# One h2T copy moved from ScalarE to VectorE, and one block of gate weights turned behind the messages of graph 1, in a two-layer graph network

## The chip, the cores and the metric

The kernel runs on one core of one Trainium2 chip. The metric is the device time of one execution in microseconds (us). In the three timed runs of the kernel before it was 2075.66, 2078.24 and 2078.29 us, median 2078.24 us. The engines are called PE (TensorE), ACT (ScalarE), DVE (VectorE), POOL (GpSimd) and SP (SyncE, which here only issues transfers); PEld is TensorE's weight load.

## The reference, cut to what matters

There are 64 graphs of 256 nodes with 256 features, all float32. `x` is (64, 256, 256), `adj` is (64, 256, 256).

```python
# layer 0
h = relu(layernorm(x))
x = x + relu(norm(adj + I) @ h @ W.T + b)
# layer 1, with h2 = relu(layernorm(x))
x_conv = relu(bn2(conv2_17_taps(relu(bn1(conv1(h2))))) + h2)
A      = exp(-dist(h2 @ w_se.T + b_se)) * adj
x_nmp  = A @ relu(h2 @ w_msg.T + b_msg)
gi     = concat(x_conv, x_nmp) @ w_ih.T + b_ih
gh     = h2 @ w_hh.T + b_hh
x = x + GRU_gates(gi, gh, h2)
```

[...] 

## The kernel before, in words

The kernel has three stages. In the first, all graphs pass through layer 0 and the first products of layer 1: `turn_adj`, `aggregate`, `project`, `turn_h`, `messages`, `conv1`, then for pairs of graphs `turn_cols`, `distance` and `pass_messages`. Beside that the weights are made ready. Then come the products of the 17-tap convolution in a transformed domain, and the gates.

Graphs 0 to 3 go through the first stage in a list written out by hand, `begin()` (lines 1165 to 1242); from graph 4 on a loop does it (line 1285). All engines keep the order of the program. Each engine's order is set by when the Python code makes its instruction: PE's instructions are made on the spot; what follows a product on another engine is put off by `after(beats, go)` (line 247) and made when `beat()` (line 559) has been called so many times more. A `beat()` also feeds the work that is paced, of which there is none this early.

These are the functions around the change:

- `turn_h(g, at, by)` (line 993): four 128x128 turns of `h2` on PE into a bank `ht`; `at` beats later `keep` copies the bank to `h2T`, and SP issues a store of it (`hTd`). `keep` uses ACT if `by` is given or paced work is waiting, else DVE.
- `messages(g)` (line 1041): eight 128x259 products `ms` from `h2T` into a bank of its own that ACT has filled with the bias first (`own_bank`, line 1014); after that DVE copies three columns (`cols`) and ACT makes `mso`. ACT fills the bank for the next graph two beats later.
- `conv1(g)` (line 1030): eight products `c` from `h2T` into another such bank, then ACT's `c1o` and a store `h1d`.
- `gate_load` and `load_part` (lines 752 and 599), called `L(w, o0)`: SP loads 256 rows of a gate matrix to a tile `nat`. `gate_turn` and `turn_away` (lines 755 and 626), called `T(w, o0)`: PE turns them, four 128x128 turns a bank, `evict` copies each bank to `w_wi` or `w_wh` (in `begin()` always on ACT), and SP stores it. `turn_away` calls `beat(0.4)` once a bank: twice for `w_ih`, once for `w_hh`. `WI` is `w_ih`, `WH` is `w_hh`.
- `later` (line 770): a list of lists of such jobs; `begin()` takes the first list between graphs 1 and 2. It is `TL(0)`, which is `taps_load` (line 645), and `L(WH, 2)`. `TL(0)` and `TL(1)` are the two loads of the raw convolution weights `w2n`, 2176 KB each, and the only loads that POOL issues. The second list gives `TL(1)`.
- `project(g)` (line 934): after its products, DVE's `pre` and `x` rows, a store `x2d`, the moments on DVE, `rs` and `nmr` on POOL, and the rows of `h2` on ACT (`norm`), two halves one beat apart.
- `load(g)` (line 819): loads of `x` and `adj` for a pair of graphs, 512 KB each.

SP issues every other load and store, one after the other in the order of the program. The program gives these transfers eight semaphores in turn, so each waits until the eighth transfer before it has landed. The tiles `nat` of 256 columns have two buffers.

The turn of the first 256 rows of `w_hh`, tile `t_wh`, stands on PE between `c` of graph 2 and `ht` of graph 3, both before and after the change.

Of the kernel before, what the change touches and what calls it, by code (L numbers as in the profile page):

```python
# [185 lines left out]
def gnn_kernel(  # L186
# [24 lines left out]
    def scratch(name, shape):  # L211
# [29 lines left out]
    pe, act, vec, pool, sp = (  # L241
        Pinned(tc, e) for e in (nc.tensor, nc.scalar, nc.vector, nc.gpsimd, nc.sync)
    )
# [3 lines left out]
    def after(beats, go):  # L247
        due.append([beats, go])

    def come_due():  # L250
        now = []
        for d in list(due):
            d[0] -= 1
            if d[0] < 0:
                now.append(d[1])
                due.remove(d)
        for go in now:
            go()
# [288 lines left out]
    with ExitStack() as one:  # L547
# [11 lines left out]
        def beat(us):  # L559
            come_due()  # L560
            paced.issue(*(k * us for k in share))

        def bank(name):
            return ps.tile([P, 512], FP, tag="ps", name=name)
# [41 lines left out]
        def turn_part(dst, nat, o0, i, tag, scale=None):  # L606

            if scale is not None:
                for k in range(2):
                    act.mul(nat[:, k, :], nat[:, k, :], scale[:, o0 + k : o0 + k + 1])  # L610
            for i0 in range(0, i // P, 2):
                t = bank(f"t_{tag}_{i0}_{o0}")
                for q in range(2):
                    for k in range(2):
                        pe.transpose(
                            t[:, (q * 2 + k) * P : (q * 2 + k + 1) * P],
                            nat[:, k, (i0 + q) * P : (i0 + q + 1) * P],
                            ident,
                        )
                after(0, lambda t=t, i0=i0: evict(  # L620
                    dst[:, i0 : i0 + 2, o0 * P : (o0 + 2) * P],
                    t.rearrange("p (q m) -> p q m", q=2),
                ))
                beat(0.4)
# [127 lines left out]
        def gate_load(tag, src, o0, i):  # L752
            nat[tag, o0] = load_part(src, o0, i, tag)

        def gate_turn(tag, dst, o0, i):
            turn_away(dst, nat.pop((tag, o0)), o0, i, tag)

        WI = ("wi", w_ih, 2 * D)
        WH = ("wh", w_hh, D)
        L = lambda w, o0: (lambda: gate_load(w[0], w[1], o0, w[2]))  # L760
        T = lambda w, o0: (lambda: gate_turn(w[0], wi_d if w is WI else wh_d, o0, w[2]))
# [75 lines left out]
        def row_moments(g, rows):  # L837
            xt, _ = st[g]["both"]
            if "mv" not in st[g]:
                st[g]["mv"] = small.tile([P, NR, 2], FP, tag="mv0", name=f"mv0_{g}", bufs=1)  # L840
            for r in rows:
                s6 = small.tile([P, 6], FP, tag="st", name=f"st0_{g}_{r}")
                vec.bn_stats(s6, xt[:, r, :])
                vec.bn_aggr(st[g]["mv"][:, r, :], s6)
# [53 lines left out]
        def turn_adj(g, at=(1, 2), by=pool):  # L898
            s = st[g]
            t = bank(f"at_{g}").rearrange("p (c i) -> p c i", c=NB)  # L900
            for jc in range(NB):
                for ic in range(NB):
                    pe.transpose(
                        t[:, jc, ic * P : (ic + 1) * P], s["at"][:, ic, jc * P : (jc + 1) * P], ident
                    )

            def keep():
                s["adjT"] = work.tile([P, NB, N], FP, tag="adjT", name=f"adjT_{g}", bufs=6)
                act.copy(s["adjT"], t)

            def hat():
                s["adjH"] = work.tile([P, NB, N], FP, tag="adjH", name=f"adjH_{g}")
                by.tensor_tensor(s["adjH"], s["adjT"], eye, ALU.add)
            after(at[0], keep)
            if at[1] is None:
                return hat
            after(at[1], hat)

        def aggregate(g):
            s = st[g]  # L920
            t = bank(f"ag_{g}").rearrange("p (c i) -> p c i", c=DC)
            for fc in range(DC):
                for jc in range(NB):
                    pe.matmul(
                        t[:, fc, :], s["hs"][:, jc, fc * P : (fc + 1) * P], s["adjH"][:, jc, :],
                        start=(jc == 0), stop=(jc == NB - 1),
                    )

            def keep():
                s["aggT"] = work.tile([P, DC, N], FP, tag="aggT", name=f"aggT_{g}")  # L930
                act.copy(s["aggT"], t)
            after(1, keep)
# [60 lines left out]
        def turn_h(g, at=1, by=None):  # L993
            s = st[g]
            t = bank(f"ht_{g}").rearrange("p (c i) -> p c i", c=DC)
            for dc in range(DC):
                for nb in range(NB):
                    pe.transpose(
                        t[:, dc, nb * P : (nb + 1) * P],
                        s["h2"][:, nb, dc * P : (dc + 1) * P],  # L1000
                        ident,
                    )

            def keep():
                s["hT"] = work.tile([P, DC, N], FP, tag="h2T", name=f"h2T_{g}")

                (act.copy if by or any(paced.lines) else vec.tensor_copy)(s["hT"], t)
                nc.sync.dma_start(hT_d[g].rearrange("p (c n) -> p c n", c=DC), s["hT"])
            after(at, keep)
# [144 lines left out]
        def stats(b):  # L1154

            g, rows = b // G * G, range(b % G * NB, (b % G + 1) * NB)
            degrees(g, rows, lambda: row_moments(g, rows))

        def scale_rows(b):
            factors(b // G * G, range(b % G * NB, (b % G + 1) * NB))  # L1160

        def rows_in(b):
            layer0_in(b // G * G, range(b % G * NB, (b % G + 1) * NB))

        def begin():

            weights_by[:] = [act.copy]
            stats(0)
            turn_adj(0, (0, 0))
            beat(0.4)  # L1170
            scale_rows(0)
            turn_part(w0T, nat_w0, 0, D, "w0")
            hat = turn_adj(1, (0, None), vec)
            beat(0.4)
            stats(1)
            hat()
            scale_rows(1)
            rows_in(0)
            turn_adj(2, (0, 0))
            beat(0.4)  # L1180
            stats(2)
            rows_in(1)
            aggregate(0)
            beat(1.7)
            turn_adj(3, (0, 1))
            scale_rows(2)
            beat(0.4)
            stats(3)
            rows_in(2)
            turn_part(wmT, nat_wm, 0, D, "wm")  # L1190
            aggregate(1)
            scale_rows(3)
            row_moments(2 * G, range(NR))
            degrees(2 * G)
            beat(1.7)
            project(0)
            beat(1.7)
            rows_in(3)
            T(WI, 0)()
            L(WI, 4)()  # L1200
            factors(2 * G)
            aggregate(2)
            beat(1.7)
            project(1)
            beat(1.7)
            small_turns()
            beat(0.1)
            aggregate(3)
            beat(1.7)
            turn_adj(4)  # L1210
            own_bank("ms", 0, bmB)
            beat(0.4)
            project(2)
            beat(1.7)
            turn_h(0, 0, act)
            small_shift()
            beat(0.4)
            turn_part(w1T, nat_w1, 0, D, "w1", scale=sc[:, 0:DC])
            own_bank("c1", 0, b1B)
            load(3 * G)  # L1220
            project(3)
            beat(1.7)
            messages(0)
            beat(1.7)
            layer0_in(2 * G, range(2))
            conv1(0)
            beat(1.7)
            T(WI, 2)()
            L(WH, 0)()
            turn_h(1, 0, act)  # L1230
            beat(0.4)
            for go in later.pop(0):
                go()
            layer0_in(2 * G, range(2, NR))
            beat(0.4)
            messages(1)
            beat(1.7)
            later.pop(0)[1]()
            later[2].insert(0, T(WI, 4))
            conv1(1)  # L1240
            beat(1.7)
            weights_by[:] = []
# [39 lines left out]
        FILTER, SPECTRA, PRODUCTS = 2, 7, 4  # L1282
        filtering = []
        begin()
        for n in range(4, B + 5):
            even, odd = n % G == 0, n % G == 1
# [391 lines left out]
```

## Time and profile before

| what | value |
|---|---|
| median of three timed runs | 2078.24 us |
| the profiled execution's own time | 2076.19 us |
| its span, first to last instruction | 2074.4 us |
| PE busy | 2029.9 us, 98% of the span |
| DVE, ACT, POOL busy | 68%, 48%, 53% |
| mean granted clock of TensorE | 0.997 |
| idle time of PE in the hundred us from 0 to 100 | 10.9 us |
| time of the change | 37 to 48 us after the span's start |

The profile is of one execution. A timeline row gives an instruction's start, its length, its engine, the line, the operation, and out<-in; rows of the same kind are merged with their number, and behind them stands how long the engine had been idle and what ended that. Nearly all instructions carry line 102, since a helper makes them, so they are told apart by the names of their tiles. The view by windows gives, for each stretch, the busy time of each engine, the granted clock of TensorE (1.00 is full) and the share of the time that the 16 DMA engines were busy.

### The profile page before, as it was taken

Reading aid. Unit: us, or ns where it says so; the run is one execution under the profiler, and the core shown is the slowest. Engines: PE = TensorE matmul, PEld = TensorE weight load, DVE = VectorE, ACT = ScalarE, POOL = GpSimd, SP = SyncE. Lnnn points to the kernel's source line nnn. Section 1 sums busy time; section 2 is a strip of 40 time slices with the busy share of each in tenths; the row PEclk is TensorE's granted clock in tenths of the full one; section 3 lists DMA queues with packets and bytes.
Section 4 is the critical chain, followed back from the end, with each engine's and each line's share of the span. In section 5 each row is a group of like instructions: output and inputs, shape, how many; then the busy total and the mean of one; then the engine's idle time right before and its main releaser. Section 6 shows DMA issues by size and latency. Waiting matters only on the chain. (4 is left out here: it accounts for less than half of the span.)

```text
span 2074.4 us, 31212 instructions
## 1 busy us (share of the span) xinstructions
PE 2029.9 (98%) x9977; PEld 1728.6 (83%) x9977; DVE 1403.6 (68%) x3172; ACT 999.2 (48%) x2171; POOL 1108.7 (53%) x1326
## 2 busy tenths in 40 slices
PE   7999999999999999999999999999999999999998
PEld 6877777888888787788888888888888888888887
DVE  5656666544688888237889815989924989965444
ACT  5756666665457676522344532234442234443333
POOL 4343333334775665347667527766626767644433
PEclk9999999999999999999999999999999999999999
DMA  8797987656765554656333455533446524322331
GB/s 282 261 259 245 265 257 248 208 178 224 240 206 198 178 178 138 212 178 204 122 117 117 137 176 190 168 101 118 124 152 199 155 92 129 116 87 89 95 96 61
DMA packets 292488, 352.84 MB, mean 170 GB/s; under 512 B 19523, under 2 KB 232150, under 8 KB 291670
## 3 DMA queue, kind: packets, MB, share of 16 engines
q1 hardware_dynamic: 292038, 346.40, 53.1%
q0 software_dynamic: 288, 4.46, 0.6%
q8 instruction: 80, 1.31, 0.3%
q14 instruction: 82, 0.67, 0.1%
HBM read 224.43 MB, written 126.35 MB: 169 GB/s over the span
## 5 line engine op out<-in xcount | busy, mean ns | idle before, releaser
L102 DVE TENSOR_TENSOR Xf<-y,k 128x256 f32<-128x256 f32 x184 | 69.0, 416 | 177.8 <-PE y L102 174.8
L102 DVE SCALAR_TENSOR_TENSOR Xf<-Xf 128x256 f32<-128x256 f32 (+1 forms) x248 | 185.1, 760 | 6.2 <-ACT Xf L102 5.1
L102 PE MATMUL ta<-T,S 128*128 128x256 f32 x768 | 186.6, 379 | 0.0
L102 PE MATMUL y<-wf,Xf 128*128 128x256 f32 x768 | 182.5, 380 | 1.8 <-DVE Xf L102 1.4
L102 POOL TENSOR_TENSOR rz<-u,p 128x256 f32<-128x256 f32 x64 | 47.8, 747 | 244.4 <-ACT u L102 244.4
L102 POOL TENSOR_TENSOR rs<-ve,mhalf 128x2 f32<-128x2 f32 x65 | 52.1, 801 | 220.0 <-DVE nm L102 218.7
L102 ACT ACTIVATE rz<-rz 128x512 f32<-128x512 f32 x128 | 80.3, 627 | 180.8 <-DVE rz L102 180.8
L102 PEld LDWEIGHTS y<-wf,Xf 128*128 128x128 f32 x768 | 143.9, 190 | 24.1 <-DVE Xf L102 2.6
L102 PEld LDWEIGHTS ta<-T,S 128*128 128x128 f32 x768 | 145.9, 190 | 19.8
L102 PE MATMUL n<-wiT,hx 128*128 128x256 f32 x512 | 152.3, 379 | 0.0
L102 POOL TENSOR_TENSOR xs<-Xf 128x256 f32<-128x256 f32 x92 | 69.8, 765 | 136.2 <-PE y L102 72.2
L102 DVE SCALAR_TENSOR_TENSOR h2l<-rz,h2l 128x256 f32<-128x256 f32 x128 | 102.9, 804 | 53.4 <-POOL h2l L102 53.4
L102 POOL TENSOR_TENSOR aT<-e,adjT 128x512 f32<-128x512 f32 x62 | 83.1, 1357 | 95.0 <-ACT e L102 95.0
L102 PE MATMUL ms<-wmT,h2T 128*128 128x259 f32 x512 | 127.2, 391 | 4.4 <-ACT h2T L102 4.4
L102 PE MATMUL n<-whT,hx 128*128 128x256 f32 x512 | 131.4, 379 | 0.0
L102 PE MATMUL n<-wiT,xcT 128*128 128x256 f32 x512 | 131.4, 379 | 0.0
L102 PE MATMUL nm<-aT,mso 128*128 128x256 f32 x512 | 123.3, 385 | 6.1 <-DVE pre L102 3.6
L102 PE MATMUL ag<-adjH,hs 128*128 128x256 f32 x512 | 124.3, 385 | 4.8 <-POOL adjH L102 2.7
L102 POOL TENSOR_TENSOR adjH<-adjT,eye 128x512 f32<-128x512 f32 x63 | 82.2, 1305 | 83.0 <-ACT adjT L102 81.2
L102 PE MATMUL o<-w0T,aggT 128*128 128x256 f32 x512 | 124.0, 385 | 1.4 <-ACT e L102 0.9
L102 PEld LDWEIGHTS ms<-wmT,h2T 128*128 128x128 f32 x512 | 97.8, 194 | 32.1 <-issue 12.9
L102 PE MATMUL c<-w1T,h2T 128*128 128x256 f32 x512 | 123.0, 383 | 0.0
(190 smaller groups left out, 5259.4 us busy)
## 6 DMA issues: line engine op xcount, KB each, us to landing
wf<-wfd SPq DMA_DIRECT2D x284, 256.0 KB
wfd<-fo SPq DMA_DIRECT2D x32, 576.0 KB
x2d<-x SPq DMA_DIRECT2D x64, 256.0 KB
h2d<-h SPq DMA_DIRECT2D x64, 256.0 KB
hTd<-h2T SPq DMA_DIRECT2D x64, 256.0 KB
h1d<-c1o SPq DMA_DIRECT2D x64, 256.0 KB
xnd<-xnT SPq DMA_DIRECT2D x64, 256.0 KB
h1l<-h1d SPq DMA_DIRECT2D x64, 256.0 KB
```

Source lines behind the costliest of these rows:

```text
L102: return self.tc.keep_in_program_order(getattr(self.engine, op)(*args, **kwargs))
```

## The change

The turn of the second block of 256 rows of `w_ih`, `T(WI, 2)`, and the load `L(WH, 0)` behind it are moved in `begin()` from in front of `turn_h(1, ...)` to behind `messages(1)`. The copy of graph 1's `h2T` loses its `act`, so that `keep` picks DVE; its place in beats becomes the next beat as before (`at` is 0).

```diff
             conv1(0)
             beat(1.7)
-            T(WI, 2)()
-            L(WH, 0)()
-            turn_h(1, 0, act)
+            turn_h(1, 0)
             beat(0.4)
             for go in later.pop(0):
                 go()
...
             beat(0.4)
             messages(1)
             beat(1.7)
+            T(WI, 2)()
+            L(WH, 0)()
             later.pop(0)[1]()
             later[2].insert(0, T(WI, 4))
             conv1(1)
```

No instruction is added or dropped. In the order of the built program the change does this. The number behind a name is the graph, or the first block of 128 rows.

| engine | before | after |
|---|---|---|
| PE | c0, t_wi, t_wi, ht1, ms1, c1, ht2 | c0, ht1, ms1, t_wi, t_wi, c1, ht2 |
| DVE | cols0, cols1 | cols0, h2T1, cols1 |
| ACT | ms1 bank, c1o0, w_wi, h2 of 2, c1 bank, w_wi, h2T1, hs, hs, h2 of 3 (two halves), mso1, ms2 bank, c1o1 | ms1 bank, c1o0, hs, hs, h2 of 2, c1 bank, h2 of 3 (half), mso1, w_wi, h2 of 3 (half), ms2 bank, w_wi, c1o1 |
| POOL | nmr2, rs3, nmr3, w2n load, w2n load | nmr2, w2n load, rs3, nmr3, w2n load |
| SP | x2d3, x8, h1d0, wid, h2d2, wid, nat_wh0, hTd1, nat_wh2, h2d3, h1d1, hTd2 | x2d3, x8, hTd1, h1d0, nat_wh2, h2d2, wid, h2d3, wid, nat_wh0, h1d1, hTd2 |

From `ht` of graph 2 on, PE's order is the same in both.

## The prediction

> **What bounds it now.** The page comes first: PE is busy 98% of the span, so the time is PE's instructions plus PE's idle time plus what is lost at a lower clock. A change that adds and drops no instruction can move only the last two. PE's timeline around the change:
>
> ```profile
> PE 2029.9 (98%) x9977; PEld 1728.6 (83%) x9977; DVE 1403.6 (68%) x3172; ACT 999.2 (48%) x2171; POOL 1108.7 (53%) x1326
> ```
> ```profile
> 35.40 1.89 PE L102 MATMUL c<-w1T,h2T 128*128 128x256 f32 x8
> 37.13 1.04 PE L102 MATMUL t_wi<-ident,nat_wi 128*128 128x128 f32 x8
> 38.00 0.60 PE L102 MATMUL ht<-ident,h 128*128 128x128 f32 x4
> 43.01 3.58 PE L102 MATMUL ms<-wmT,h2T 128*128 128x259 f32 x8 [4.41 <-ACT h2T L102]
> 46.37 2.06 PE L102 MATMUL c<-w1T,h2T 128*128 128x256 f32 x8
> 48.27 0.60 PE L102 MATMUL ht<-ident,h 128*128 128x128 f32 x4
> ...
> 57.36 0.60 PE L102 MATMUL t_wh<-ident,nat_wh 128*128 128x128 f32 x4
> ```
>
> PE stands still for 4.41 us, its longest wait, until ACT has copied h2T of graph 1. Behind that, ms takes 3.36 us from its start to that of c, where the next graph's takes 1.84 (51.31 to 53.15). The windows show why: a low clock after the wait.
>
> ```profile
> 39.88:43.29 3.41, 0.28 (x1) 0.29 (x2) 0.00 (x0) 3.41 (x8) 0.62 (x2) 1.00 0.99 301
> 43.29:46.71 3.42, 3.42 (x9) 2.70 (x9) 0.02 (x1) 1.62 (x4) 0.00 (x0) 0.50 1.00 399
> 142.28:145.69 3.41, 1.29 (x8) 0.98 (x7) 1.68 (x5) 0.09 (x1) 0.00 (x0) 1.00 1.06 378
> 145.69:149.10 3.41, 3.41 (x10) 2.63 (x9) 3.22 (x13) 3.41 (x9) 0.90 (x2) 0.50 1.07 393
> ```
>
> The columns are the stretch, its length, busy time of PE, PEld, DVE, ACT and POOL, granted clock, DMA share and GB/s. Twice a stretch of 3.41 us with PE busy for 0.28 or 1.29 us is followed by one at clock 0.50. Where PE was busy 1.94 us (797.64 to 801.05) the next one kept 1.00. So a wait costs its length, and another 1.7 us if most of such a stretch falls into it. Last, the DMA share is 0.99 to 1.06 here: transfers have a queue of their own to stand in.
>
> **Step 1, the copy.** In the new order ht1 follows c0 at 37.13 and ends at 37.73. DVE's rows run without a gap up to cols0, whose last reduction ends at 38.78. A DVE copy of h2T takes 0.69 us (row at 48.91), so it is done at 39.47. ms1 also needs its bank, which ACT fills from 39.39 for 0.59 us, to 39.98; that is the later one. With the 0.06 us that the trace has between copy and product, ms1 starts at 40.04 instead of 43.01. Then come ms 1.84, the eight turns t_wi 0.87 (37.13 to 38.00) and c1 1.73 (35.40 to 37.13): ht2 starts at 44.48 instead of 48.27, **3.79 us earlier**. The two ACT evictions and SP's stores of w_wi move behind and hold nobody: the banks that they free are asked for by `at` of graph 5 and by di, at 47.1 and 49.4. ACT has hs, the other half of h2 of graph 2 and c1's bank in front of c1: five pieces of 0.5 from 39.91, done at 42.5, and c1 comes at 42.75. If the clock drops after this shorter wait of 2.3 us, 1.7 of the 3.79 are lost.
>
> **Step 2, the load behind it.** From ht2 on PE's order is unchanged, and it ran 9.09 us without a wait to t_wh at 57.36. Moved up by 3.79, t_wh is asked for at 53.57. What has slack of less? DVE, ACT and POOL rows move along, since PE releases them. Transfers do not. t_wh reads nat_wh0, the load of the moved `L(WH, 0)`. It was the fifth transfer behind x8 on SP and becomes the eighth: hTd1, h2d3 and nat_wh2 now stand in front.
>
> ```profile
> 42.91 0.52 SPq L102 DMA_DIRECT2D nat_wh<-in_L_gnn_w_hh_dram  x1
> 43.52 3.93 SPq L1008 DMA_DIRECT2D hTd<-h2T  x1
> 47.54 3.45 SPq L102 DMA_DIRECT2D nat_wh<-in_L_gnn_w_hh_dram  x1
> ...
> 54.89 0.33 SPq L1008 DMA_DIRECT2D hTd<-h2T  x1
> 55.59 0.59 SPq L831 DMA_DIRECT2D adj<-in_adj_dram  x1
> ```
> ```profile
> DMA to landing us min/median/max: 9.2/11.8/14.4
> ```
> ```profile
> q0 software_dynamic: 143, 2.21, 87.6%
> q1 hardware_dynamic: 126, 0.26, 11.0%
> ```
>
> Already before, nat_wh0 was nearly late. SP's waits say that hTd2 at 54.89 waited for the landing of the first wid and adj at 55.59 for that of h2d2, each eight places in front: 0.7 us a transfer. nat_wh0 is two places behind h2d2, so it landed at about 55.5 + 2 x 0.7 = 56.9 at the latest, and PE's weight load for t_wh began at 57.1. The reason is the second fence (landing times of the two w2n loads) and the third (queues from 44 to 50 us): POOL's two loads, issued at 39.14 and 40.0 and landed by 40.0 + 14.4 = 54.4 (the first by 39.1 + 9.2 = 48.3), hold the DMA engines. In those 6 us both queues got through some 21 packets per us, but POOL's are 17 KB and SP's 1 or 2 KB, so SP's queue got 0.26 of 2.48 MB. When POOL's are done, SP's queue moves 392 GB/s (1.96 MB in 55 to 60 us), 0.67 us for 256 KB.
>
> The change moves this too. The first w2n load is no longer behind nmr3 (39.20) but behind nmr2, which ends at 36.10: 3.0 us earlier, in front of SP's x2d3 (issued 36.90) and x8 (37.31), which before had the engines to themselves until 40. If POOL's queue keeps its rate it ends 3.0 us earlier, at about 51.3. Until then x2d3 (256 packets of 1 KB at 21 per us, 12 us from 38) is all that SP's queue gets done. Then x8 needs 512 KB, 1.3 us, to 52.6, and eight transfers of 0.67 us follow, to 58.0. From the other side, POOL's last packets may thin out a us before the last landing, as 0.67 DMA share and 239 GB/s in 53 to 54 us show, and nat_wh0 lands at 57.0. I take 57.5. t_wh's products follow 0.26 us behind its weight load: 57.8, against 57.36. **The 3.79 us are gone, and 0.4 more.** The order of SP alone (three places, 2.0 us, with POOL's queue as before) would give 58.9; POOL's earlier start alone gives back some of it.
>
> **Step 3, the clock.** PE now waits from 53.6 to 57.5, about 4 us. A stretch of 3.41 us that has 1.7 or more of that always exists, and by the two rows above the next is at half clock. Before, the 4.41 us wait cost 1.52 in ms and 0.17 in c, 1.69 in all. It depends on where the wait falls in the 3.41 us grid: 0.5 if PE still waits in half of the slow stretch, 1.7 if it works through it. I take 1.6, as the row. The first wait, 2.3 us, may drop the clock as well, but that would be made up while PE waits for t_wh anyway. [...]
>
> **Sum.** +0.4 for t_wh and +1.6 for the clock: 2.0 us more than the profiled execution's 2076.19, 2078.2. That execution was 2.05 us under the median of the runs, 2078.24, so I predict 2078.24 + 2.0 = **2080.2 us**. After t_wh nothing else is late: w2n of block 0, used by ACT at about 52.4, lands earlier than before; the store hTd1 that frees h2T for graph 3 lands three places sooner; x8 is read by DVE only at 70.7.
>
> About 0.2% (4.15 us) is what a measurement of this kernel can tell from no change.
>
> **Rivals.**
> - *The load comes in part earlier* (17%). SP's x2d3 and x8 slip through while POOL's first packets are being made (before, the first w2n issue was at 39.14 and the window 41 to 42 still had a DMA share of 0.18). Against the central case that is up to 0.75 MB, 1.9 us: t_wh at 55.9, the wait 2.3 us, with or without the clock's 1.7: -1.5 to +0.2.
> - *The change does what it says* (11%): nat_wh0 is not late, PE keeps 3.79 us: 2074.4. For it: no row of before shows PE waiting for a transfer here. Against it: 0.2 us of slack in a DMA share of 1.0.
> - *Slower beyond doubt* (10%): POOL's queue ends no earlier than before, at 54.3, because its second load is issued at 39.14 as before and the first one's packets, sent with SP's in turn, only stretch. Then x8 and the eight end at 54.3 + 1.3 + 5.4 = 61.0, t_wh is at 61.3, and with the clock it is 3.9 + 1.6 = +5.5: 2083.7. It is over 0.2% once nat_wh0 lands after 59.6.
> - The central case has 62%, with a range of its own of -0.4 + 0.5 to +0.9 + 1.7, 2078.3 to 2080.8; the runs of before differ by 2.6 us, which I add below.
>
> **Numbers.** The range takes the central and the partial case (2078.24 - 1.5, less 1.1 for half of the runs' spread, is 2075.6) and reaches towards the slower one, to +4.8: 2083.0; what is left out is the full gain and the worse part of the slower case, 16%. Faster by over 0.2% needs 4.15 us, more than the whole 3.79, so it is 7%, out of the second rival and the spread of the runs; slower by over 0.2% 11%; within 82%.
>
> **What would show it.** Right if ms1 starts at 40.0 with an idle time of 2.3 us that DVE or ACT's bank ends; ht2 at 44.5; the first w2n issue at 36.1; and a new wait of PE in front of t_wh of 3 to 5 us, released by nat_wh's load, with clock 0.50 behind it. Wrong if t_wh follows c2 without a gap, or if the wait stands there and ht3 starts before 57.

## The result, and the profile after

The changed kernel takes 2080.31 us (median of 20 runs, 2078.76 to 2082.48), the kernel before in the same runs 2077.62 us (20 runs, 2074.66 to 2079.33). The ratio is 1.0016, with a 95% interval of 1.0010 to 1.0022: 2.7 us slower in the medians, 3.3 by the ratio, 2.1 to 4.6 by its interval. The profiled execution took 2081.67 us with a span of 2079.9 us.

PE's busy time is as before, and so is its share; what changed is where it waits. These are the profile's line on the engines, and PE's timeline of the same stretch:

```profile
PE 2029.2 (98%) x9977; PEld 1728.1 (83%) x9977; DVE 1403.2 (67%) x3173; ACT 998.5 (48%) x2170; POOL 1108.7 (53%) x1326
```
```profile
35.38 1.89 PE L102 MATMUL c<-w1T,h2T 128*128 128x256 f32 x8
37.11 0.60 PE L102 MATMUL ht<-ident,h 128*128 128x128 f32 x4
40.02 2.02 PE L102 MATMUL ms<-wmT,h2T 128*128 128x259 f32 x8 [2.31 <-ACT ms L102]
...
44.47 0.60 PE L102 MATMUL ht<-ident,h 128*128 128x128 f32 x4
...
51.83 1.89 PE L102 MATMUL c<-w1T,h2T 128*128 128x256 f32 x8
58.69 1.09 PE L102 MATMUL t_wh<-ident,nat_wh 128*128 128x128 f32 x4 [4.97 <-DMA nat_wh<-in_L_gnn_w_hh_dram]
```

The reader is to see three things. The wait in front of ms1 is 2.31 us instead of 4.41, and it is ACT's filling of the bank that ends it, no longer the copy. Up to ht2 PE is 3.80 us ahead (44.47 against 48.27). Then a wait of 4.97 us stands in front of t_wh, where none was, released by a transfer; t_wh starts 1.33 us later than before (58.69 against 57.36).

The windows after that wait, with the columns as before (the granted clock is the third number from the end):

```profile
52.78:56.20 3.42, 0.94 (x5) 0.49 (x3) 3.22 (x7) 3.42 (x4) 1.96 (x2) 1.00 1.07 375
56.20:59.61 3.41, 0.92 (x5) 0.95 (x6) 0.24 (x2) 1.75 (x3) 2.90 (x5) 0.50 1.08 393
59.61:63.02 3.41, 3.41 (x12) 2.87 (x11) 1.38 (x2) 0.00 (x0) 0.20 (x1) 0.50 0.66 229
63.02:66.44 3.42, 3.42 (x19) 3.03 (x18) 0.00 (x0) 2.68 (x6) 0.68 (x1) 1.00 0.70 214
```

The wait covers most of two stretches (0.94 and 0.92 us of work in them); behind the first of them two are at clock 0.50, the second one full of work (3.41 us). From t_wh to nm of graph 0 PE needs 5.19 us (58.69 to 63.88) instead of 3.04 (57.36 to 60.40): 2.15 us. With the 1.33 us of t_wh that makes 3.48 us, and the distance between the two traces stays at 3.5 us up to 140 us. The rest of the 5.5 us between the spans comes later, from waits that differ from execution to execution (the wait of nm for DVE at about 145 us is 3.5 us here, 2.1 in the profile before, 1.6 to 3.3 in those of the experiments).

What stood in front of the load is seen in SP's issues, in the landing of the two w2n loads, and in the queues from 40 to 46 us:

```profile
36.88 0.36 SPq L954 DMA_DIRECT2D x2d<-x  x1
37.30 0.46 SPq L830 DMA_DIRECT2D x<-in_x_dram  x1
...
41.98 5.32 SPq L981 DMA_DIRECT2D h2d<-h  x1
...
50.68 0.36 SPq L641 DMA_DIRECT2D wid<-w_wi  x1
52.59 0.37 SPq L102 DMA_DIRECT2D nat_wh<-in_L_gnn_w_hh_dram  x1
```
```profile
DMA to landing us min/median/max: 8.5/9.9/11.2
```
```profile
q0 software_dynamic: 154, 2.40, 93.9%
q1 hardware_dynamic: 121, 0.12, 5.8%
```

POOL issues its first w2n load at 36.02 instead of 39.14, before x2d3. In the 6 us from 40 on SP's queue gets 0.12 of 2.53 MB. The last two issues tell when the transfers eight places in front landed, since SP's waits name them: the second wid (the row at 50.68) waited for x2d3, until about 50.6, and nat_wh0 for x8, until about 52.5. In the kernel before these two had landed at 39.16 and 41.02, and POOL's first packets came between 40 and 41. nat_wh0 is then the eighth behind x8. The trace keeps 16 landings for nat_wh0, as for each of SP's transfers around it; I call them its parts: 15 of them land by 57.87, the last one at 58.55. In the kernel before all 16 had landed by 56.87.

### The profile page after: what moved, and what is told of

Its sections match the earlier page's. It is cut to its first block, busy times and chain, and to the rows that moved or that the text cites. A ratio compares the mean times of both kernels' runs of the same rounds, so it can differ in the third digit from the quotient of the medians.

```text
span 2079.9 us, 31212 instructions
## 1 busy us (share of the span) xinstructions
PE 2029.2 (98%) x9977; PEld 1728.1 (83%) x9977; DVE 1403.2 (67%) x3173; ACT 998.5 (48%) x2170; POOL 1108.7 (53%) x1326
```

## The experiments

The theory: PE gains the 3.8 us, and loses more than that because nat_wh0 comes late; it is late by its place on SP's queue, and that queue stands still while POOL's two loads run. Rivals: the gain isn't there for another reason; POOL's earlier load, not the place on SP, makes it late; or it is the place on SP at any load of POOL's. As a measure that is free of the start of the execution, I give how long after the start of c0 nm of graph 0 starts: 25.00 us before (35.40 to 60.40), 28.50 in the changed kernel (35.38 to 63.88). Where t_wh has been moved behind nm (e4, e5, e11), its own 0.43 us have to be added.

### One place of the load back: e1_load_early

```diff
+            L(WH, 0)()
             turn_h(1, 0)
...
             T(WI, 2)()
-            L(WH, 0)()
```

> The changed kernel, with the load of the first block of w_hh issued again in front of the turn of graph 1 (it stands on SP behind x2d3 and in front of x8); POOL's first w2n load stays early. Theory (the load of nat_wh0 is late by its place on SP, behind POOL's two large loads): x2d3 is through when POOL's loads end at about 50.4, nat_wh0 follows at about 51.1, t_wh is asked for at 53.6 and does not wait; ht of graph 3 starts at 54.0, PE stays 3.8 us ahead of the kernel before, about 2073.8 us against a median before of 2077.6. Rival (the earlier h2T copy gains nothing, something other than the load holds PE): a wait of some 4 to 5 us stays in front of t_wh or of ht of graph 3, and the time stays at about 2080.

Measured: 2075.36 us against 2076.88, ratio 0.9991 (0.9982 to 1.0000). The wait in front of t_wh is gone. But PE is 2.1 us ahead (22.91 us from c0 to nm), not 3.8. The windows of this kernel show the rest:

```profile
37.38:40.80 3.42, 1.11 (x7) 0.78 (x6) 1.82 (x10) 2.43 (x5) 1.46 (x3) 1.00 1.03 332
40.80:44.21 3.41, 3.41 (x13) 2.83 (x12) 0.59 (x4) 2.96 (x7) 0.00 (x0) 0.50 1.01 428
```

The 2.3 us wait in front of ms1 lies whole in one stretch, and the next one is at clock 0.50, which costs 1.7: from ms1 to c1 it is 4.41 us (39.99 to 44.40), in the changed kernel 2.72 (40.02 to 42.74). So the theory on the load holds; the size was missed, since no second wait hides what the clock takes behind the first one.

### POOL's load back: e2_taps_late

```diff
-            for go in later.pop(0):
-                go()
+            taps_0, rows_2 = later.pop(0)
+            rows_2()
...
+            taps_0()
             later.pop(0)[1]()
```

> The changed kernel, with POOL's first w2n load put back behind nmr3, as in the kernel before; SP's order as in the changed kernel. Theory A (the three places on SP make nat_wh0 late; POOL's earlier start gives nearly as much as it takes): POOL's loads end at 54.3, nat_wh0 lands at 56.5 + 3 x 0.67 = 58.5, t_wh starts at 58.8, as in the changed kernel (58.7), time 2080. Theory B (POOL's earlier start is what makes it late): nat_wh0 lands at 56.5 to 57.1, t_wh at 57.0 to 57.4, the wait is 3.5 us, time about 2079.

Measured: 2081.51 us against 2076.88, ratio 1.0022 (1.0014 to 1.0031). PE's timeline of it:

```profile
59.52 1.09 PE L102 MATMUL t_wh<-ident,nat_wh 128*128 128x128 f32 x4 [6.36 <-DMA nat_wh<-in_L_gnn_w_hh_dram]
```

t_wh starts 24.69 us after c0 (34.83); in the changed kernel it is 23.31, before 21.96. So the three places on SP alone cost 2.7 us, and POOL's earlier start gives back 1.4 of them. Theory B, that the earlier start makes the load late, falls. Theory A has the cause, but its time was missed: it had nat_wh0 landing at 58.5 and t_wh where the changed kernel has it, and POOL's start gives back half of the three places, not nearly all. (Here, too, one part of 16 lands last, at 59.39, the others by 58.72.)

### The copy alone: e3_copy_alone

```diff
             T(WI, 2)()
             L(WH, 0)()
-            turn_h(1, 0, act)
+            turn_h(1, 0)
```

> The kernel before, with only the copy of h2T of graph 1 moved to DVE; the turn of w_ih and the load of w_hh stay where they were. Theory (the load bounds this stretch, wherever PE's gain comes from): ms1 starts at 40.0, c1 follows at once, ht2 at 43.6, t_wh is asked for at 52.7 but nat_wh0 lands at about 56.5 as in the kernel before; t_wh at 56.8, a wait of 4 us, then a lower clock for 1.7 to 2.1 us: +1.3 us on the kernel before, about 2079. Rival (only the move of the load makes it late): t_wh at 52.7 without a wait, 4.6 us ahead, about 2073.

Measured: 2079.05 us against 2076.88, ratio 1.0011 (1.0002 to 1.0020). The copy alone is slower, too:

```profile
39.69 2.02 PE L102 MATMUL ms<-wmT,h2T 128*128 128x259 f32 x8 [1.44 <-ACT ms L102]
...
57.58 1.09 PE L102 MATMUL t_wh<-ident,nat_wh 128*128 128x128 f32 x4 [4.83 <-DMA nat_wh<-in_L_gnn_w_hh_dram]
```

Here nat_wh0 has its old place, and PE waits 4.83 us for it all the same. In the kernel before, that wait was covered by PE's own wait for ACT's copy. 14 of its 16 parts land by 56.19, where the expectation had 56.5, but the last two only at 57.45. The turns of w_ih fill part of the gap in front of ms1 here, so that wait is 1.44 us.

### The reader of the load moved: e4_turn_later

```diff
-            [S(0, 0), S(0, 1), S(0, 2), S(0, 3), T(WH, 0), L(WH, 4)],
-            parts[0][0:5] + [S(1, 0), S(1, 1), gate_biases_load],
+            [S(0, 0), S(0, 1), S(0, 2), S(0, 3)],
+            parts[0][0:5] + [S(1, 0), S(1, 1), T(WH, 0), L(WH, 4), gate_biases_load],
```

> The changed kernel, with the turn of the first block of w_hh (and the load of its third block behind it) one graph later on PE; all loads up to it as in the changed kernel. Theory: nat_wh0 lands at 58.4 as in the changed kernel, but nobody asks for it before about 65, so ht of graph 3 starts at 53.6, there is no wait and no lower clock, PE stays 3.8 us ahead of the kernel before: about 2073.8. Rival (the wait at 53.6 stands for something else, such as the DMA share of 1.0 in general): another wait of several us appears between 53 and 62, time 2078 to 2080.

Measured: 2073.07 us against 2076.88, ratio 0.9984 (0.9975 to 0.9992): 3.8 us faster than the kernel before in the medians, and some 6.5 better than the changed one, each against the kernel before in its own runs. From 42 to 100 us PE stands still for 0.15 us in all. So what the change was about is there; it was kept from the end by one transfer. The clock stays at 1.00 in this profile, though the wait in front of ms1 is 2.3 us again: the stretch with that wait holds 1.60 us of work.

```profile
37.56:40.97 3.41, 1.60 (x7) 1.42 (x8) 1.09 (x6) 3.23 (x7) 1.46 (x3) 1.00 0.84 348
40.97:44.39 3.42, 3.42 (x23) 3.06 (x23) 0.59 (x4) 3.42 (x8) 0.00 (x0) 1.00 1.02 431
```

### The copy and the reader, or the copy and the load: e5 and e6

e5 is e3 with e4's edit. In e6 the load stands right behind x2d3 on SP, ahead of POOL's loads:

```diff
+            L(WH, 0)()
             layer0_in(2 * G, range(2))
             conv1(0)
             beat(1.7)
             T(WI, 2)()
-            L(WH, 0)()
-            turn_h(1, 0, act)
+            turn_h(1, 0)
```

> The kernel before, with only the copy of h2T of graph 1 on DVE (as in e3_copy_alone), and with the turn of the first block of w_hh and the load of its third block one graph later on PE. The turn of w_ih stays in the gap in front of ms1. Theory: the wait in front of ms1 is 1.4 us as in e3_copy_alone, too short to lower the clock; ht2 starts 4.7 us earlier than in the kernel before, nobody waits for nat_wh0, and the time is 4.5 us under the kernel before, about 2072.4 against 2076.9, a little under e4_turn_later, whose wait of 2.3 us drops the clock in some executions. Rival (e4 gained from moving the turns of w_ih, not from the copy): no more than 2 us under the kernel before.

> The kernel before, with only the copy of h2T of graph 1 on DVE, and with the load of the first block of w_hh issued on SP right behind x2d3, in front of x8 and about 2 us before POOL's first w2n load is issued; its turn stays where it was. Theory (only the landing of nat_wh0 stands between the copy and its gain): nat_wh0 lands at about 40 to 41, t_wh is asked for at 52.7 and does not wait; 4.5 us under the kernel before, as e5_copy_and_turn_later. Rival (POOL's loads hold back some other transfer that PE needs in these 10 us): a new wait between 44 and 60, and no gain over 2 us.

Measured: e5 2074.18 us, ratio 0.9985 (0.9976 to 0.9994); e6 2073.62 us, ratio 0.9981 (0.9973 to 0.9990); the kernel before 2077.46. Neither waits for nat_wh0, both have 1.4 us in front of ms1. But the 4.5 us are not all there, since a new wait stands a little behind, as e5's waits show, of PE first and of DVE second:

```profile
PE ms L102 <- DVE h2T L102: 2.5, 1, 2.5
```
```profile
DVE h2T L102 <- DMA hTd<-h2T: 3.0, 1, 3.0
```

DVE's copy of h2T of graph 3 takes the buffer of graph 1, and that is free once the store hTd1 has landed. hTd1 stands behind the stores of w_ih here; SP issues it from 42.76 to 46.74, and the copy that its landing releases starts at 58.41. In e6 the wait of ms is 0.7 us. My rival for e6 was right in this: POOL's loads hold back another transfer that PE needs; its time, no gain over 2 us, was not (3.8). The rival for e5, no more than 2 us if the copy gains nothing, falls as well (3.3).

### The wait filled: e7_filled_wait

```diff
+        def fill():
+            t = bank("fill")
+            for k in range(36):
+                pe.transpose(t[:, k % 4 * P : (k % 4 + 1) * P], ident, ident)
...
-            [S(0, 0), S(0, 1), S(0, 2), S(0, 3), T(WH, 0), L(WH, 4)],
+            [S(0, 0), S(0, 1), S(0, 2), S(0, 3), fill, T(WH, 0), L(WH, 4)],
```

> The changed kernel, with 36 more 128x128 turns of the identity in front of t_wh (3.9 us of work on PE into a bank that nobody reads). Theory (half of what the change costs is the lower clock behind the wait): t_wh still starts at about 58.6, since it waits for nat_wh0, but the clock stays 1.00, and nm of graph 0 starts at 61.7 instead of 63.9; the time is about 2.1 us under the changed kernel, 1.3 us over the kernel before, about 2078.2. Rival (the clock drop costs nothing, or is made up later): as the changed kernel, about 2080.

Measured: 2079.43 us against 2077.46, ratio 1.0010 (1.0001 to 1.0019). In this profile the clock dropped behind ms1's wait already (ms1 takes 3.47 us to the next product, 39.91 to 43.38, where the changed kernel has 1.85), so the filling came late and left no wait:

```profile
55.07 4.09 PE L102 MATMUL fill<-ident 128*128 128x128 f32 x36
59.00 0.60 PE L102 MATMUL t_wh<-ident,nat_wh 128*128 128x128 f32 x4
```

From t_wh to nm of graph 0 it is 3.04 us (59.00 to 62.04), as before, against 5.19 in the changed kernel. So the trace gives the clock 2.15 us. The medians can't tell 1.0010 from 1.0016.

### The turns moved, the copy on ACT: e8_turns_moved_copy_on_act

```diff
-            turn_h(1, 0)
+            turn_h(1, 0, act)
```

> The second half of the change alone: the turn of w_ih and the load of w_hh behind the messages of graph 1, but the copy of h2T of graph 1 stays on ACT. Theory (t_wh's start is set by the load, so the copy's engine makes no difference to the time): ACT's copy is its next piece behind c1o0, done at 41.0; ms1 starts at 41.05, ht2 at 45.5, t_wh is asked for at 54.6 and starts at 58.7 as in the changed kernel; time as the changed kernel, 2080. Rival (the time follows ms1): 1.0 us over the changed kernel.

Measured: 2080.35 us against 2077.46, ratio 1.0012 (1.0003 to 1.0021), not to be told from the changed kernel's 1.0016; but the interval leaves room for the rival's 1.0 us, too. In its profile PE was early (c0 at 33.28), and waited 4.67 us for ACT's copy and 0.90 us for nat_wh0:

```profile
40.28 3.82 PE L102 MATMUL ms<-wmT,h2T 128*128 128x259 f32 x8 [4.67 <-ACT h2T L102]
...
57.87 0.63 PE L102 MATMUL t_wh<-ident,nat_wh 128*128 128x128 f32 x4 [0.90 <-DMA nat_wh<-in_L_gnn_w_hh_dram]
```
```profile
39.55:42.96 3.41, 2.68 (x6) 2.18 (x7) 0.00 (x0) 3.16 (x7) 0.00 (x0) 0.50 0.99 404
42.96:46.37 3.41, 3.41 (x13) 2.94 (x12) 0.59 (x4) 1.95 (x4) 0.00 (x0) 0.50 1.02 432
```

Behind the first wait the clock was halved for two stretches: from ms1 to ht2 PE needed 7.43 us (40.28 to 47.71) instead of the changed kernel's 4.45, so 3.0 us more. All the same t_wh is at 57.87, since the load lands at 57.73. So in this profile what PE loses ahead of the load is taken out of its wait for the load. That the engine of the copy makes no difference while the load is late fits this; the medians alone don't show it.

### What stands still, and the two best versions: e9, e10, e11

e9 is e6 with `turn_h(1, 0)` in front of `T(WI, 2)()`, so that hTd1 stands in front of the stores of w_ih; e11 is e5 with the same. e10 is the changed kernel with POOL's second load later:

```diff
-            later.pop(0)[1]()
+            later.pop(0)
...
-            [S(0, 0), S(0, 1), S(0, 2), S(0, 3), T(WH, 0), L(WH, 4)],
+            [TL(1), S(0, 0), S(0, 1), S(0, 2), S(0, 3), T(WH, 0), L(WH, 4)],
```

> The kernel before, with the copy of h2T of graph 1 on DVE, the turn of graph 1 in front of the turns of w_ih (which so still fill the gap in front of ms1), and the load of the first block of w_hh issued right behind x2d3. So the store hTd1 stands in front of the stores of w_ih on SP. Theory (in e6 the copy of h2T of graph 3 waited for the landing of hTd1, which frees its buffer): the wait of ms3 for h2T goes, t_wh does not wait, the wait in front of ms1 stays 1.4 us; nm of graph 0 starts 20.1 to 20.6 us after c0 (before: 25.0; changed kernel: 28.5); time 4.5 to 5 us under the kernel before, about 2072.5. Rival (that wait has another cause): ms3 still waits 0.7 to 2.5 us for h2T.

> The changed kernel, with POOL's second w2n load issued some 14 us later (between the two aT of graphs 0 and 1); orders of PE and SP as in the changed kernel. Theory (SP's queue stands still because POOL's two loads share the DMA engines with it packet by packet): POOL's first load alone lands at about 44, from then on SP's queue has the engines to itself, nat_wh0 lands at about 50 although it is still the eighth behind x8, t_wh is asked for at 53.6 and does not wait; PE stays 3.8 us ahead of the kernel before, 2.1 if the clock drops behind the wait of ms1: 2073 to 2075. Rival (the eight places on SP are what counts, at any load of POOL's): t_wh still waits 3 us or more, time about 2080.

> As e5_copy_and_turn_later, with the turn of graph 1 in front of the turns of w_ih, so that the store hTd1 stands in front of the stores of w_ih on SP; nothing else differs. Theory: in e5 DVE's copy of h2T of graph 3 waited 3.0 us for the landing of hTd1; now hTd1 lands at about 50, four transfers sooner, and the wait of 2.5 us in front of ms3 goes: about 2 us under e5, 2072. Rival: the wait stays, time as e5, 2074.

Measured, the kernel before at 2077.92: e10 2075.42 us, ratio 0.9988 (0.9979 to 0.9997). With the orders of PE and SP as in the changed kernel, t_wh follows c2 without a wait:

```profile
51.43 1.89 PE L102 MATMUL c<-w1T,h2T 128*128 128x256 f32 x8
53.16 0.60 PE L102 MATMUL t_wh<-ident,nat_wh 128*128 128x128 f32 x4
```
```profile
q1 hardware_dynamic: 1940, 2.13, 103.3%
```

The second fence is its queues from 44 to 50 us: SP's queue moves 2.13 MB, where it got 0.26 in the kernel before. So the eighth place costs nothing once POOL's second load is away. It is not the place that makes the wait, since e3 has it at the old, fifth place as well: behind x8 and POOL's two loads nat_wh0 is late at either place, and the three places make it later. The margin is small: nat_wh0 lands at 52.20, not at 50 as expected, 1 us before t_wh. nm starts 21.22 us after c0, 3.8 us ahead; the medians gain 2.5 us (0.6 to 4.4 by the interval).

e9 takes 2073.22 us, ratio 0.9977 (0.9967 to 0.9987), e11 2072.33 us, ratio 0.9975 (0.9966 to 0.9984). In both the wait of ms3 is gone; nm starts 20.59 and 20.13 us after c0. They beat the kernel before by 4.7 and 5.6 us, and the changed one as well. The intervals of e4, e5, e6, e9 and e11 overlap, and the traces put none of the two first: with t_wh's 0.43 us e11's nm would stand at 20.56, and ht of graph 4 starts 29.60 us after c0 in e9 and 29.91 in e11 (before: 34.01).

## Why the prediction was right

The forecast was 2080.2 us, no change that a measurement tells or a little slower. The mechanism of the central case came true: the gain of the copy is there, it is lost in front of t_wh, and the clock drops behind that wait. Both of its costs were too small, by more than the central case allowed for (+1.33 us for t_wh and 2.15 for the clock, where it had at most 0.9 and 1.7). That 2080.2 and the measured 2080.31 agree to 0.1 us is luck: the kernel before came out 0.6 us faster in the later runs than the median that the forecast started from. With 20 runs each the interval is 0.12% wide, so the change is told from none, though it is less than the 0.2% of the prediction.

- **Step 1, the copy: right.** ms1 at 40.02 (forecast 40.04), the wait 2.3 us, ended by ACT's bank as forecast, ht2 at 44.47 (44.48), and t_wh would have been next at 53.56 (c2 starts at 51.83 and takes 1.73 to the next product; forecast 53.57).
- **Step 2, the load: right in its mechanism, 0.9 us too small.** nat_wh0 landed at 58.55, not 57.5, and t_wh started at 58.69, not 57.8. POOL's queue ended at 36.02 and 39.16 plus 8.5 to 11.2, so by 50.4, even 0.9 us sooner than I took. x8 then needed 1.9 us instead of 1.3 (DMA moved 249 and 306 GB/s in the us from 50 and 51, not 392) and landed at 52.53, where the sum had 52.6. For 15 of the 16 parts the eight transfers took 5.34 us, as the 5.4 of the sum, so that nat_wh0 would have landed at 57.87. My sum, 58.0, was right to 0.13 us; averaging it with a lower one took 0.5 off. What the sum lacked is the last part, 0.68 us behind the others. The lag shows first in the transfer whose other parts land by 53.82; at 52.70 a packet of the instruction queue (16 KB, 0.97 us) had started. In the kernel before no packet of that size and queue runs from 36 to 60 us, and nat_wh0 has no lag. That the packet causes the lag fits, but no run tests it. That POOL's earlier start gives back some 1.4 us (58.9 to 57.5) is what e2 shows against the changed kernel.
- **Step 3, the clock: right in its mechanism, 0.55 us too small.** 2.15 us instead of 1.6. The wait of 4.97 us left 0.94 and 0.92 us of work in two stretches, and the one of 0.92, at clock 0.50 itself, was followed by another at 0.50. That a clock drop behind ms1's wait would be covered by the second wait is not seen in the changed kernel's profile, whose clock stayed at 1.00 there (ms1 takes 1.85 us to the next product). e8 shows such a cover, and e1, without it, lost the 1.7 us.
- **The sum** was +2.0, the trace has +3.5 at 64 us, the medians +2.7, the ratio +3.3 (2.1 to 4.6). The low end of the range took 1.1 us for half of the runs' spread of 2.6, which is 1.3; it changes nothing here.
- **"Nothing else is late"** holds for the changed kernel. For the better versions it doesn't: hTd1 was next (e5, e6). I had named that store, and its place in the changed order is why it didn't show there.
- **The rivals.** That the full gain comes was wrong, and e4, e10 and e11 show what it needed. That x2d3 and x8 slip through, so that the load comes in part earlier, was wrong: from 38 to 41 us SP's queue got 1 packet against POOL's 54, and x2d3 landed only at 50.62. The slower rival (POOL's queue ends no earlier) was wrong: it ended 4.0 us earlier, at 50.4 against 54.4. Its second load was not issued as before either, but at 39.16 instead of some 40.0.

## What to carry to other kernels

When PE stops waiting for an engine, what it asks for next comes sooner by as much, but a transfer does not: look for the first instruction behind the gain that reads a load, and work out its landing from the queue in front of it. Here the load landed 0.49 us before its use (56.87 and 57.36), which covered little of the 3.8. Look also at what another queue moves while the moved transfer stands: with POOL's loads at 94% of the DMA time (from 40 to 46 us) SP's queue got 0.12 of 2.53 MB, and the three places cost 2.7 us (e2), where 0.67 us a transfer makes 2.0. Then move either the reader, the load, or the large loads: each of the three took the wait away here (e4, e1, e10). The reader and the large loads brought a clear gain; the load alone brought 1.5 us, with 1.0000 at the edge of its interval, since the clock of 0.50 behind ms1's wait took 1.7 us back.

## What the runs showed of the hardware

- In the changed kernel POOL's queue got 154 packets and SP's 121 in the 6 us from 40; in the kernel before it was 143 and 126 in the 6 us from 44. POOL's loads had packets of 17 KB, SP's were of 1 KB (of 2 KB in the kernel before). POOL's queue had 94% of the DMA time (88% before), SP's 6% (11%).
- At the start of the large loads SP's queue got even less: 1 packet against 54 from 38 to 41 us, and in the kernel before none against 50 from 41 to 44, with transfers issued and waiting. Why is not shown.
- Stretches of 3.41 us with 0.28 and 1.29 (kernel before), 0.94 (changed kernel), 1.11 and 1.50 us (e1) of PE's work in them were followed by one at clock 0.50; those with 1.47 (e5), 1.60 (e4) and 1.94 (kernel before) by one at 1.00. The two closest are these, of e1 (the next stretch is at 0.50) and of e5 (the next is at 1.00):

```profile
139.79:143.20 3.41, 1.50 (x10) 1.20 (x9) 1.57 (x4) 0.00 (x0) 0.00 (x0) 1.00 1.08 338
```
```profile
55.18:58.59 3.41, 1.47 (x7) 0.95 (x5) 0.42 (x3) 3.38 (x7) 2.90 (x5) 1.00 1.07 394
```

- Those two are 44% and 43% of a stretch, and the one with more work is the one behind which the clock was 0.50; so in these runs PE's work in a stretch does not tell the next one's clock to the last few per cent. By where it fell, the same 2.3 us wait was followed by 0.50 in e1 (1.11 us of work in its stretch) and by 1.00 in e4 (1.60 us).
- Stretches at clock 0.50 with 0.92 (changed kernel, 56.20 to 59.61) and 2.68 us (e8, 39.55 to 42.96) of PE's time in them were followed by another at 0.50, one with 3.41 us (changed kernel, 59.61 to 63.02) by one at 1.00.
- With 36 useless turns in the wait (e7) PE took 3.04 us from t_wh to nm of graph 0, against 5.19 in the changed kernel: 2.15 us less behind it.
